# Finer hand-over of a feed-forward beside chains and attention, other leads at two borders, and a forward transform by pairs of slabs

## The chip, the cores and the metric

The kernel runs on one core of a Trainium2 chip. A core has a matrix engine (TensorE, PE in the profile; its weight loads are listed apart as PEld), a vector engine (DVE), a scalar engine (ACT), GpSimd (POOL) and SyncE (SP), which issues most of the transfers. Each engine works through its own queue of instructions in order and waits at semaphores for the others. The metric is the time of one execution on the device in microseconds (us); lower is better.

## The reference

The input x has 4 batches, 512 time steps (T) and 128 x 64 = 8192 features (D), in float32. Two layers follow each other. Cut to what is computed:

```
# layer 0, for each batch
xn = layernorm(x)                                 # over D
k, v, r = xn @ Wk, xn @ Wv, sigmoid(xn @ Wr)      # 64 states
s[t] = decay * s[t-1] + k[t] * v[t]               # a scan over time
x  = x + (r * s) @ Wo
x  = x + gelu(conv(layernorm(x)) + freq_b)        # 3 taps over the 128, 64 x 64 channels
x  = x + layernorm(causal_conv(layernorm(x)))     # 3 taps over time, per feature
x  = x + gelu(x @ W1 + b1) @ W2 + b2              # 64 -> 256 -> 64
# layer 1, for each batch
trend = moving_average(x, 25)                     # over time, ends repeated
xs    = rfft(x - trend)[:128]                     # over time
ys    = einsum(xs, w_real + i * w_imag)           # a 128 x 128 complex matrix per channel
out   = trend + irfft(ys)
```

## The kernel before

**Layer 0** keeps features on the 128 partitions and the 512 time steps along the free axis. A batch has 64 chunks of 128 features, handled in 32 pairs (`NPR`). The work of a batch is written as Python generators, which emit instructions and yield a weight after each step:

- J, `project`: products with Wk, Wv, Wr for all pairs (L407), and the row statistics on DVE (L339).
- Z, `scan`: a chain of short steps, each of which needs the result of the one before. Two rows of scale and mean are spread over the partitions (`rows`, L241 on PE, L285 on ACT), then k and v (L468, L472), r (L476), the scan, and two products (L494, L502/L503) for the next statistics, which end in a power on POOL (L233).
- A, `attend_and_convolve`: two more rows, then for each pair the product with Wo and the sum with x (L527, L529, L533), the convolution (L548 to L563), and sums for the next norm (`add_up`, L251).
- C, `convolve_time`, O, `open_feed`: the causal convolution and its norm; its rows are again chains. `convolve_ahead` does the first 14 pairs of the next batch's convolution early, within F (L611 to L630).
- F, `feed_forward`: for each pair four quarters. `widen(i, q)` is one quad of four 64x64 matmuls (L730) and a GELU on ACT (L735). `narrow(i, q)` is a quad (L743) that accumulates over the quarters into two PSUM banks; after the fourth quarter DVE adds the residual (L756). `store` transposes a finished pair (eight 128x128 transposes, L762), ACT copies it out (L770/L775) and POOL stores every second one (L771). `residual` and `add_residual` (L689, L690, L698, L701) prepare the pair after next.

A step that belongs to a chain yields `CHAIN` (6.0). F yields once per pair.

What TensorE does in which order is fixed by the program (`manual_schedule`); the other engines are ordered by a scheduler that starts from the program's order. `in_turn` sets this order: it walks through eight couples of generators, and takes the next step from the one that is behind. `leads` holds, for each border between couples, by which share of a couple the second generator is to be ahead, and is interpolated in between:

```
((0, (O, 0.05), (F, 0.95)), (2, (J, 0.88), (Z, 0.12))),   # couple 2
((1, (C, 1.0)), (2, (A, 1.0))),                           # couple 3
((1, (O, 0.05), (F, 0.95)), (3, (J, 0.88), (Z, 0.12))),   # couple 4
((2, (C, 1.0)), (3, (A, 1.0))),                           # couple 5
((2, (O, 0.05), (F, 0.95)), (3, (C, 0.95), (O, 0.05))),   # couple 6
((3, (F, 1.0)), (3, (nothing, 1.0))),                     # couple 7
```

A may run three steps beside a running F; at its fourth it is held until F is done, because both need the same PSUM bank.

**Layer 1** takes the batches in twos. For each: `transform` of both, `mix`, `invert` of both. `transform` walks over 16 slabs of 512 features (`SL`). A slab is loaded as `xin`, 128 partitions by four blocks of 512 (L921, five buffers). DVE forms sum and difference of its halves (`uv`, L938) and sum and difference of the first (`ev`, L943). PE multiplies the difference with `dftd` (L947, 128x64 tiles), `ev` with `dftv` (L954, 128x32 tiles), and 24 rows from both ends of time, `edge`, with `dfte` (L961, 24 rows, 64 columns). `edge` is loaded by two POOL transfers (L932, L933) and doubled by ACT (L934). ACT copies the two PSUM banks to `xf` (L963). `mix` (L981, L985) needs all slabs of both batches. The pools give `edge`, `uv0`, `uv1` and `ev` two buffers each, and each of the two PSUM names `a` and `b` four banks.

Of the kernel before, what the change touches and what calls it, by code (L numbers as in the profile page):

```python
# [10 lines left out]
F32 = mybir.dt.float32  # L11
AF = mybir.ActivationFunctionType
ALU = mybir.AluOpType
# [66 lines left out]
def layer0(ctx, tc, dram, x, xt, vecs, wkvr, wo, wdec, wconv, fbias, w1, fb1, w2, fb2, x4):  # L80
# [236 lines left out]
    free_s = [True]  # L317
    feeding = [False]
    held = [False]
    unscanned = [True]  # L320


# [389 lines left out]
    def feed_forward(b):  # L712
# [8 lines left out]
        def unit():  # L721
            turn[0] ^= 1
            return two(ps_m, "m") if turn[0] else c_bank()

        def widen(i, q):
            x3 = x3s[i]
            pm = unit()
            for h in range(2):
                for j in range(2):
                    nc.tensor.matmul(  # L730
                        pm[halves[j], h, :], lhsT=w1_sb[halves[h], q * H : (q + 1) * H], rhs=x3[halves[h], j, :],
                        start=True, stop=True,
                    )
            mid = mids[i, q] = bk.tile([P, 2, SL], F32, tag="mid", name="mid", bufs=4)
            nc.scalar.activation(mid, pm, AF.Gelu_apprx_tanh, bias=fb1_sb[:, q : q + 1])  # L735

        def narrow(i, q):
            if q == 0:
                sums2[i] = of_p(), ps_s.tile([P, SL], F32, tag="s", name="pb")
            mid = mids.pop((i, q))  # L740
            for h in range(2):
                for j in range(2):
                    nc.tensor.matmul(  # L743
                        sums2[i][j][halves[h], :], lhsT=w2_sb[halves[j], q, :], rhs=mid[halves[j], h, :],
                        start=q == 0, stop=q == 3,
                    )
            if q < 3:
                return
            x3 = x3s.pop(i)
            if lag > 1:  # L750
                pair = spare("wx", 4 * S + SL)[:, :, 0:SL]
                x4s[i] = [pair[:, j, :] for j in range(2)]
            else:
                x4s[i] = [bk.tile([P, SL], F32, tag="x4t", name="x4t", bufs=3) for _ in range(2)]
            for j, pa in enumerate(sums2.pop(i)):
                nc.vector.scalar_tensor_tensor(x4s[i][j], pa, fb2_sb, x3[:, j, :], ALU.add, ALU.add)  # L756
# [18 lines left out]
                nc.scalar.copy(o, pt)  # L775

        early = None
        widen(0, 0)
        widen(0, 1)
        for i in range(NPR + lag):  # L780
            if i >= lag:
                store(i - lag)
            if i < NPR:
                widen(i, 2)
                narrow(i, 0)
                widen(i, 3)
                narrow(i, 1)
                if i + 2 < NPR:
                    coming = residual(b, i + 2)
                if i + 1 < NPR:  # L790
                    widen(i + 1, 0)
                narrow(i, 2)
                if i + 1 < NPR:
                    widen(i + 1, 1)
                if i + 2 < NPR:
                    x3s[i + 2] = add_residual(b, i + 2, *coming)
                narrow(i, 3)
            if b + 2 < B and i > 1:
                early = early or convolve_ahead(b + 1, lambda: unit()[:, 0, :])
                next(early, None)  # L800
            yield 9.0 * (NPR + 1) / (NPR + lag)
        feeding[0] = False


# [5 lines left out]
    def run(b, stages):  # L810
        for stage, share in stages:
            for weight in stage(b):
                yield BLOCKED if weight == BLOCKED else weight * share / whole[stage]

    def in_turn(leads, *pairs):
        at, running = [0.0, 0.0], [None, None]
# [54 lines left out]
def layer1(ctx, tc, x4, wri, dftv, dftd, dfte, idfte, idfto, avg, avgh, out):  # L871
# [53 lines left out]

    def transform(b, xf):

        for s in range(NS):
            c = slice(s * SL, (s + 1) * SL)
            xin = slab(b, s)  # L930
            edge = io.tile([P, SL], F32, tag="edge", name="edge")
            nc.gpsimd.dma_start(edge[0:HALO, :], x4[b][0:HALO, c])  # L932
            nc.gpsimd.dma_start(edge[HALO : 2 * HALO, :], x4[b][T - HALO : T, c])  # L933
            nc.scalar.copy(edge[32 : 32 + 2 * HALO, :], edge[0 : 2 * HALO, :])  # L934
            uv = []
            for op in (ALU.add, ALU.subtract):
                t = io.tile([P, 2, SL], F32, tag=f"uv{len(uv)}", name="uv")
                nc.vector.tensor_tensor(t, xin[:, 0:2, :], xin[:, 2:4, :], op)  # L938
                uv.append(t)
            pf = [bank("a"), bank("a")]  # L940
            ev = io.tile([P, 2, SL], F32, tag="ev", name="ev")
            for k, op in enumerate((ALU.add, ALU.subtract)):
                nc.vector.tensor_tensor(ev[:, k, :], uv[0][:, 0, :], uv[0][:, 1, :], op)  # L943
            for i in range(2):
                for r in range(2):
                    h = 1 - r
                    nc.tensor.matmul(  # L947
                        pf[r][h * H : (h + 1) * H, :], lhsT=dftd_sb[:, i, r, :], rhs=uv[1][:, i, :],
                        start=(i == 0), stop=False,
                    )  # L950
            for k in range(2):
                for r in range(2):
                    q = r * H + k * H // 2
                    nc.tensor.matmul(  # L954
                        pf[r][q : q + H // 2, :], lhsT=dftv_sb[:, k, r, :], rhs=ev[:, k, :], start=True, stop=False
                    )
            for r in range(2):
                at = slice(32 * r, 32 * r + 2 * HALO)
                for h in range(2):
                    hs = slice(h * H, (h + 1) * H)  # L960
                    nc.tensor.matmul(pf[r][hs, :], lhsT=dfte_sb[at, hs], rhs=edge[at, :], start=False, stop=True)  # L961
            for r in range(2):
                nc.scalar.copy(by_c(xf[:, r, c]), by_n(pf[r]))  # L963

    def mix(xf):

# [93 lines left out]
def _constants():  # L1060
# [28 lines left out]
    for j, s in enumerate(tiles):  # L1089
# [77 lines left out]
```

## Time and profile before

| | us |
|---|---|
| median of three runs (range) | 3747.47 (3742.09 to 3767.47) |
| profiled execution | 3753.95 |
| its span in the profile | 3752.0 |
| TensorE busy | 3572.1 (95%) |
| VectorE busy | 2676.7 (71%) |
| ScalarE busy | 1762.1 (47%) |
| GpSimd busy | 512.5 (14%) |

Moved through DMA: 913.39 MB, 243 GB/s over the span. The mean granted TensorE clock is 0.975.

Busy time is the union of an engine's instructions; for TensorE the ends are modelled, and a matmul that runs at half clock counts as busy for twice as long. A line of the busy view by stretches gives the stretch, its length, busy us and number of instructions of each engine, the granted clock, the mean busy share of the 16 DMA engines and GB/s. A line of the waits gives who waited for whom, us in total, how often, and the longest. A line of the timeline gives start, duration, engine, line of the code, what is written from what, tile, shape and number of records; a float32 matmul has two records. Behind it, in brackets, stands how long the engine was idle before and what released it.

### The profile page before, as it was taken

How to read it: one execution, taken by the hardware profiler on the slowest of the kernel's cores; microseconds unless marked ns; L12 is line 12 of the kernel's file. 1: busy time of each engine (PE TensorE's matmuls, PEld its weight loads, DVE VectorE, ACT ScalarE, POOL GpSimd, SP SyncE). 2: the span in 40 equal slices, each digit the busy share in tenths (PEclk: the TensorE clock that was granted, in tenths of full speed). 3: DMA queues.
4: the chain of work that ended last, by engine and by line, in shares of the span. 5: the costliest groups of instructions: out<-in, count | busy, mean ns of one | idle time of the engine just before them, and what ended most of it. 6: DMA issues, size and time to landing. Idle time of an engine off the chain costs nothing. (4 is left out here: it accounts for less than half of the span.)

```text
span 3752.0 us, 52992 instructions
## 1 busy us (share of the span) xinstructions
PE 3572.1 (95%) x20041; PEld 1376.3 (37%) x20041; DVE 2676.7 (71%) x3498; ACT 1762.1 (47%) x2299; POOL 512.5 (14%) x782
## 2 busy tenths in 40 slices
PE   9989999999998999999899899999989999999998
PEld 4433322234333223433322333333323833327533
DVE  4445669977776895777689699846667277882677
ACT  0023346656665565666556578868844200142100
POOL 0000012210111221011122121100012000131010
PEclk9999999999998999999889999999999999999999
DMA  9867657787883787788478577645577478983687
GB/s 314 271 211 245 230 187 252 260 275 269 292 286 135 260 286 277 259 292 291 144 249 282 198 256 259 223 159 192 193 247 243 154 247 293 326 277 139 212 289 264
DMA packets 429206, 913.39 MB, mean 243 GB/s; under 512 B 33240, under 2 KB 83608, under 8 KB 424856
## 3 DMA queue, kind: packets, MB, share of 16 engines
q1 hardware_dynamic: 351024, 636.87, 51.6%
q0 software_dynamic: 75776, 271.62, 20.0%
q8 instruction: 160, 2.62, 0.3%
q10 hardware_dynamic: 2152, 1.51, 0.1%
q14 instruction: 94, 0.77, 0.1%
HBM read 641.37 MB, written 268.50 MB: 243 GB/s over the span
## 5 line engine op out<-in xcount | busy, mean ns | idle before, releaser
L743 PE MATMUL p<-mid,w_sb 64*64 64x512 f32 x2048 | 559.1, 596 | 15.5 <-DVE wx L756 14.3
L743 PE MATMUL pb<-mid,w_sb 64*64 64x512 f32 x2048 | 531.6, 596 | 0.7 <-DVE wx L756 0.7
L735 ACT ACTIVATE mid<-c,fb_sb 128x1024 f32<-128x1024 f32 x256 | 284.4, 1111 | 91.4 <-PE c L730 90.9
L735 ACT ACTIVATE mid<-m,fb_sb 128x1024 f32<-128x1024 f32 x256 | 284.8, 1112 | 88.6 <-PE m L730 87.3
L730 PE MATMUL c<-x,w_sb 64*64 64x512 f32 x2016 | 280.8, 610 | 16.1 <-ACT mid L735 11.9
L730 PE MATMUL m<-x,w_sb 64*64 64x512 f32 x2016 | 280.7, 609 | 6.7 <-ACT mid L735 4.5
L743 PEld LDWEIGHTS p<-mid,w_sb 64*64 64x64 f32 x2048 | 158.7, 135 | 287.8 <-issue 248.9
L407 PE MATMUL a<-xp,wx 128*128 128x512 f32 x512 | 238.7, 609 | 0.5 <-DVE me L268 0.5
L1012 ACT COPY two<-a 128x512 f32<-128x512 f32 x64 | 37.5, 586 | 426.6 <-PE a L1007 426.6
L1035 PE MATMUL b<-xin,avg_sb 128*128 128x512 f32 x512 | 230.8, 593 | 3.1 <-DVE xin L1041 3.1
L1041 DVE TENSOR_TENSOR xin<-b,pm 128x512 f32<-128x512 f32 x256 | 159.0, 683 | 97.8 <-PE b L1038 82.8
L568 ACT ACTIVATE sq<-x 128x1024 f32<-128x1024 f32 x128 | 135.0, 1055 | 173.4 <-DVE x L565 173.4
L623 DVE SCALAR_TENSOR_TENSOR to<-kd,vec,to 128x510 f32<-128x510 f32 (+1 forms) x272 | 197.1, 742 | 12.5 <-ACT to L619 11.2
L698 ACT ACTIVATE kd<-kd,vec 128x512 f32<-128x512 f32 x256 | 192.8, 803 | 3.1 <-DVE kd L690 3.1
L917 DVE COPY xf<-b 128x256 f32<-128x256 f32 x128 | 54.3, 424 | 185.4 <-PE b L981 173.3
L251 PE MATMUL st<-x,ones 128*32 128x512 f32 x512 | 168.9, 605 | 11.5 <-DVE x L565 11.5
L529 DVE TENSOR_TENSOR x<-a,xp 128x1024 f32<-128x1024 f32 x128 | 156.0, 1218 | 32.7 <-PE a L527 30.5
L623 DVE SCALAR_TENSOR_TENSOR z<-x,vec,z 128x511 f32<-128x511 f32 x240 | 175.9, 744 | 4.4 <-ACT z L619 2.8
L938 DVE TENSOR_TENSOR uv<-xin 128x1024 f32<-128x1024 f32 x128 | 154.6, 1224 | 32.5 <-PE a L947 15.6
L701 DVE TENSOR_TENSOR x<-kd,kx 128x1024 f32<-128x1024 f32 x126 | 154.0, 1222 | 32.5 <-ACT kd L698 32.5
L527 PE MATMUL a<-rst,wo_sb 64*128 64x512 f32 x512 | 150.7, 663 | 25.8 <-DVE x L529 22.5
L756 DVE SCALAR_TENSOR_TENSOR x4t<-p,fb_sb,x 128x512 f32<-128x512 f32 x64 | 47.9, 748 | 177.2 <-PE pb L743 177.1
(259 smaller groups left out, 6849.8 us busy)
## 6 DMA issues: line engine op xcount, KB each, us to landing
xp<-in_xt SPq DMA_DIRECT2D x256, 512.0 KB
xin<-x SPq DMA_DIRECT2D x128, 1024.0 KB
kh<-to SPq DMA_DIRECT2D x156, 512.0 KB
x<-x POOLq DMA_DIRECT2D x128, 512.0 KB, 4.4
kx<-x SPq DMA_DIRECT2D x128, 512.0 KB
x<-ob POOLq DMA_DIRECT2D x64, 1024.0 KB, 8.3
out<-xin POOLq DMA_DIRECT2D x64, 1024.0 KB, 6.3
x<-x SPq DMA_DIRECT2D x96, 512.0 KB
```

What stands on the lines that cost most here:

```text
L251: nc.tensor.matmul(st[32 * q : 32 * q + 32, :], lhsT=ones, rhs=src[:, j, :], start=first, stop=last,)
L407: nc.tensor.matmul(pa[:, k, :], lhsT=wq[:, j, k * P : (k + 1) * P], rhs=xp[:, j, :], start=first and j == 0, stop=last and j == 1,)
L529: nc.vector.tensor_tensor(x1, at, xp, ALU.add)
L623: tap = nc.vector.scalar_tensor_tensor(to[:, j, k:], xr[:, j, : SL - k], vec[:, w, c], to[:, j, k:], ALU.mult, ALU.add)
L698: tc.keep_in_program_order(nc.scalar.activation(d[:, j, :], d[:, j, :], AF.Identity, bias=vec[:, B4, c], scale=vec[:, G4, c]))
L701: nc.vector.tensor_tensor(x3, d, x2, ALU.add)
L730: nc.tensor.matmul(pm[halves[j], h, :], lhsT=w1_sb[halves[h], q * H : (q + 1) * H], rhs=x3[halves[h], j, :], start=True, stop=True,)
L735: nc.scalar.activation(mid, pm, AF.Gelu_apprx_tanh, bias=fb1_sb[:, q : q + 1])
L743: nc.tensor.matmul(sums2[i][j][halves[h], :], lhsT=w2_sb[halves[j], q, :], rhs=mid[halves[j], h, :], start=q == 0, stop=q == 3,)
L938: nc.vector.tensor_tensor(t, xin[:, 0:2, :], xin[:, 2:4, :], op)
L1035: nc.tensor.matmul(po[j], lhsT=avg_sb[:, j, :], rhs=xin[:, j, :], start=True, stop=False)
L1041: nc.vector.tensor_tensor(by_n(xin[:, j, :]), by_n(po[j]), by_c(pm[j % 2][:, j // 2, :]), ALU.add)
```

## The change

- **F by quarters.** The steps of a pair are the same, with `residual` now before the quarter's `narrow`. F collects weight in `done` by quarters of 2.25 and yields at the end of a pair, or after each quarter as long as the set `narrowly` isn't empty. `run` puts a stage in that set when it yields `CHAIN` or when it is A, and takes it out at another weight or at its end.
- **Leads.** At the borders before couple 3 and before couple 5 the second generator (A of batch 2 and of batch 3) is to be 0.1 ahead in place of 0.04 and 0.02.
- **Transform.** The loop goes over pairs of slabs. The loads and the DVE sums of both are emitted, then the `dftd` matmuls of both, the `dftv` matmuls of both, the `edge` matmuls of both, and four copies. One `edge` tile holds both slabs' rows, at partitions 0 and 64, so the four groups of 24 rows start at 0, 32, 64 and 96; the constant `dfte` is doubled to 128 rows for this. The difference is formed before the sum. Groups use the banks `a` and `b` in turn, four banks each.

```diff
+    narrowly = set()
 ...
         early = None
+        done = 0.0
+        quarter = 2.25 * (NPR + 1) / (NPR + lag)
         widen(0, 0)
         widen(0, 1)
         for i in range(NPR + lag):
             if i >= lag:
                 store(i - lag)
-            if i < NPR:
-                widen(i, 2)
-                narrow(i, 0)
-                widen(i, 3)
-                narrow(i, 1)
-                if i + 2 < NPR:
-                    coming = residual(b, i + 2)
-                if i + 1 < NPR:
-                    widen(i + 1, 0)
-                narrow(i, 2)
-                if i + 1 < NPR:
-                    widen(i + 1, 1)
-                if i + 2 < NPR:
-                    x3s[i + 2] = add_residual(b, i + 2, *coming)
-                narrow(i, 3)
-            if b + 2 < B and i > 1:
-                early = early or convolve_ahead(b + 1, lambda: unit()[:, 0, :])
-                next(early, None)
-            yield 9.0 * (NPR + 1) / (NPR + lag)
+            for q in range(4):
+                done += quarter
+                if i < NPR:
+                    if q < 2:
+                        widen(i, q + 2)
+                    elif i + 1 < NPR:
+                        widen(i + 1, q - 2)
+                    if i + 2 < NPR and q == 1:
+                        coming = residual(b, i + 2)
+                    if i + 2 < NPR and q == 3:
+                        x3s[i + 2] = add_residual(b, i + 2, *coming)
+                    narrow(i, q)
+                if q == 3 and b + 2 < B and i > 1:
+                    early = early or convolve_ahead(b + 1, lambda: unit()[:, 0, :])
+                    next(early, None)
+                if q == 3 or narrowly:
+                    yield done
+                    done = 0.0
 ...
             for weight in stage(b):
+                if weight == CHAIN or stage is attend_and_convolve:
+                    narrowly.add((stage, b))
+                elif weight != BLOCKED:
+                    narrowly.discard((stage, b))
                 yield BLOCKED if weight == BLOCKED else weight * share / whole[stage]
+            narrowly.discard((stage, b))
 ...
-            (0.12, 0.12, 0.08, 0.04, 0.08, 0.02, -0.05, 0.08, 0.0),
+            (0.12, 0.12, 0.08, 0.1, 0.08, 0.1, -0.05, 0.08, 0.0),
 ...
-        for s in range(NS):
-            c = slice(s * SL, (s + 1) * SL)
-            xin = slab(b, s)
+        for g in range(NS // 2):
             edge = io.tile([P, SL], F32, tag="edge", name="edge")
 ...
+            uv, ev, pf = [], [], []
+            for k in range(2):
+                s = 2 * g + k
+                c = slice(s * SL, (s + 1) * SL)
+                xin = slab(b, s)
+                q = k * H
+                nc.gpsimd.dma_start(edge[q : q + HALO, :], x4[b][0:HALO, c])
+                nc.gpsimd.dma_start(edge[q + HALO : q + 2 * HALO, :], x4[b][T - HALO : T, c])
+                nc.scalar.copy(edge[q + 32 : q + 32 + 2 * HALO, :], edge[q : q + 2 * HALO, :])
+                u = io.tile([P, 2, SL], F32, tag="uv0", name="u")
+                v = io.tile([P, 2, SL], F32, tag="uv1", name="v")
+                nc.vector.tensor_tensor(v, xin[:, 0:2, :], xin[:, 2:4, :], ALU.subtract)
+                nc.vector.tensor_tensor(u, xin[:, 0:2, :], xin[:, 2:4, :], ALU.add)
+                t = io.tile([P, 2, SL], F32, tag="ev", name="ev")
+                for i, op in enumerate((ALU.add, ALU.subtract)):
+                    nc.vector.tensor_tensor(t[:, i, :], u[:, 0, :], u[:, 1, :], op)
+                uv.append(v)
+                ev.append(t)
+                pf.append([bank("ab"[g % 2]), bank("ab"[g % 2])])
+            for k in range(2):
+                for i in range(2):
+                    for r in range(2):
+                        h = 1 - r
+                        nc.tensor.matmul(
+                            pf[k][r][h * H : (h + 1) * H, :], lhsT=dftd_sb[:, i, r, :], rhs=uv[k][:, i, :],
+                            start=(i == 0), stop=False,
+                        )
 ...
+            for k in range(2):
+                for r in range(2):
+                    at = slice(k * H + 32 * r, k * H + 32 * r + 2 * HALO)
+                    for h in range(2):
+                        hs = slice(h * H, (h + 1) * H)
+                        nc.tensor.matmul(
+                            pf[k][r][hs, :], lhsT=dfte_sb[at, hs], rhs=edge[at, :], start=False, stop=True
+                        )
 ...
-        "dfte": dfte.reshape(2 * 32, M),
+        "dfte": np.concatenate([dfte.reshape(2 * 32, M)] * 2),
```

More of the change, by code (lines that the diff above doesn't have):

```diff
@@ L926, in transform @@
     def transform(b, xf):
-        for s in range(NS):
-            c = slice(s * SL, (s + 1) * SL)
-            xin = slab(b, s)
+        for g in range(NS // 2):
             edge = io.tile([P, SL], F32, tag="edge", name="edge")
[L932 to L950, printed above, removed]
@@ new lines, in transform @@
+            for k in range(2):
[7 more added lines that the diff above has]
+            for k in range(2):
+                for i in range(2):
+                    for r in range(2):
+                        q = r * H + i * H // 2
+                        nc.tensor.matmul(
+                            pf[k][r][q : q + H // 2, :], lhsT=dftv_sb[:, i, r, :], rhs=ev[k][:, i, :],
+                            start=True, stop=False,
+                        )
@@ L951, in transform @@
             for k in range(2):
                 for r in range(2):
[L953 to L961, printed above, removed]
@@ L962, in transform @@
-            for r in range(2):
-                nc.scalar.copy(by_c(xf[:, r, c]), by_n(pf[r]))
+                    at = slice(k * H + 32 * r, k * H + 32 * r + 2 * HALO)
+                    for h in range(2):
+                        hs = slice(h * H, (h + 1) * H)
+                        nc.tensor.matmul(
+                            pf[k][r][hs, :], lhsT=dfte_sb[at, hs], rhs=edge[at, :], start=False, stop=True
+                        )
+            for k in range(2):
+                s = 2 * g + k
+                for r in range(2):
+                    nc.scalar.copy(by_c(xf[:, r, s * SL : (s + 1) * SL]), by_n(pf[k][r]))
```

## The prediction

> **What bounds the kernel now.** I began with the page's first two parts.
>
> ```profile
> span 3752.0 us, 52992 instructions
> ...
> PE 3572.1 (95%) x20041; PEld 1376.3 (37%) x20041; DVE 2676.7 (71%) x3498; ACT 1762.1 (47%) x2299; POOL 512.5 (14%) x782
> ...
> PE   9989999999998999999899899999989999999998
> ...
> PEclk9999999999998999999889999999999999999999
> ```
>
> TensorE is the bound: 95% busy, the next engine at 71%. Only two things are left to take from it: its 180 us of idle time, and time in which it is busy but slow. So I asked where the granted clock falls, by stretches of the busy view:
>
> ```profile
> 1150.00:1240.00 90.00, 71.53 (x400) 30.58 (x402) 53.57 (x75) 41.20 (x49) 11.65 (x16) 0.79 0.38 130
> 1800.00:1900.00 100.00, 79.40 (x474) 31.50 (x466) 62.52 (x84) 49.34 (x59) 11.21 (x16) 0.80 0.37 130
> ...
> 2762.00:2893.00 131.00, 129.17 (x768) 30.81 (x764) 112.26 (x125) 55.67 (x94) 36.48 (x70) 0.98 0.92 305
> 3250.00:3387.00 137.00, 133.83 (x770) 31.76 (x768) 113.93 (x128) 56.01 (x96) 39.49 (x73) 0.96 0.87 288
> ```
>
> Columns: stretch, its length, busy us of PE, PEld, DVE, ACT and POOL, granted clock, DMA share, GB/s. The first two are the borders where a feed-forward F ends, the scan Z of a later batch runs and its attention A begins. Idle is 18.5 and 20.6 us. By slices of 10 us, busy time times (1 - clock) is a further 14.3 and 15.5 us. A border thus loses about 33 to 36 us, 69 us for both. The waits of the second border and two rows of its timeline (start, duration) say why:
>
> ```profile
> PE a L494 <- DVE rst L489: 7.1, 1, 7.1
> PE a L241 <- POOL rs L233: 5.2, 2, 3.3
> PE a L468 <- DVE wx L472: 3.4, 1, 3.4
> ...
> 1819.45 1.16 PE L241 MATMUL a<-ident,mean 128*128 128x128 f32 x8
> ...
> 1870.14 2.08 PE L241 MATMUL a<-ident,rs 128*128 128x128 f32 x8 [3.34 <-POOL rs L233]
> ```
>
> Each step of the scan needs a DVE or POOL result of the step before. Two scan steps stand back to back, with the whole pair of F (8.2 us) before or after both. After a gap the same eight transposes take 2.08 in place of 1.16 us.
>
> The last two stretches are the forward transforms of two batches each, 32 slabs in 131.8 us (2761.6 to the mix's first matmul at 2893.3) and in 136.7 us (3250.3 to 3387.0). One slab in the steady part:
>
> ```profile
> 2853.77 1.94 PE L947 MATMUL a<-uv,dftd_sb 128*64 128x512 f32 x8
> ...
> 2855.64 1.07 PE L954 MATMUL a<-ev,dftv_sb 128*32 128x512 f32 x8
> 2855.75 1.22 DVE L938 TENSOR_TENSOR uv<-xin 128x1024 f32<-128x1024 f32 x1 [0.19 <-PE a L947]
> ...
> 2856.63 1.09 PE L961 MATMUL a<-edge,dfte_sb 24*64 24x512 f32 x8
> ...
> 2857.65 1.94 PE L947 MATMUL a<-uv,dftd_sb 128*64 128x512 f32 x8
> ```
>
> Start to start, a slab costs PE 1.87 + 0.99 + 1.02 = 3.88 us, and DVE waits for PE to free `uv`. Where DVE runs freely its slabs start at 2800.76, 2804.36 and 2807.96: 3.60 us. DMA moves 305 GB/s there at share 0.92, and 376 GB/s in the first 20 us of the stage.
>
> **What the Trainium skill says.** "TensorE: Matmul & The Clock Gate", Part 1, has the array at half clock after an idle window of about 3.4 us; 1.16 against 2.08 us agrees. "TensorEngine Tiling (Array Packing)", Key Properties, says that a change of tiling mode drains the array. The trace agrees: quads of one shape follow each other at 0.86 us, and the slab's L954, the same 512 columns, costs 0.99 where shapes change, so about 0.14 us each. The tiling page's list of configurations has eight tiles of 32x64; before shows four of them side by side (8 records of L961 in 1.09 us), not eight.
>
> **Part 1: quarters and leads.** F does the same matmuls; only its hand-over is finer while the partner is in a chain or in A. The planned order of the changed kernel puts this between the steps at both borders (quad w or n: 0.86 us, eight transposes T: 1.05): first row, 2.8 us, second row, 3.4, first k/v, 6.2, second k/v, 3.4, r, 4.5, L494, 6.2, L502, 3.4, row, 6.2, row, 7.9, first L527. Against this the delays of before, from the end of a step to the start of what it frees:
> - k/v to k/v 3.4 (cover 6.2): 0 left. k/v to r 4.1 (3.4): 0.7. r to L494 7.05 (4.5): 2.6.
> - L494 to L502/L503 about 4.5 (6.2): 0. L502 to the row 5.2 (3.4): 1.8. Rows to L527 1.4 or less: 0.
> - Unchanged: first row 1.7 (the scan still follows the last projection at once), one L527 behind L529 1.3, waits for GELU about 2.
> - New: the last T stands right behind the last n and waits for two L756, 1.5; and 10 more changes of tile shape at 0.15, 1.5.
>
> Together 13 us, and 2 for one cold window (the 2.6 could set one off): 15 against 34.5, so **-19.5 per border, -39 for both**. Moved along: A's first three steps with `xp` and `wo_sb` loads on SP, 3 x 2.44 us on DVE (L529, L533) and `scaled` on ACT come into F's tail. Queued behind them are F's last L756 and L735, for which the last n and T wait. DVE is at 63% there, so nothing beyond the 1.5; without that room two adds, 2.4 us a border. DVE and SP also meet J's statistics and loads in another order earlier in F. PE is at 98 to 99% from 900 to 1100, so I take nothing; bounds -3 to +6. In F2 beside C3 a second row comes two quads earlier, before a 3.0 us wait for GELU at 2154: zero, +-4.
>
> **Part 2: two slabs together.** Same matmul count. Per pair of slabs: eight concurrent edge matmuls in one slot take away 1.02, and the modes change 3 times, not 6: 3 x 0.14. PE: 2 x 3.88 - 1.02 - 0.42 = 6.3 us. If eight tiles don't run together it is 7.3. DVE keeps its instructions: 2 x 3.60 = 7.2. So DVE becomes the bound either way, and 0.28 us a slab is what the steady part can give.
>
> First stage: the second slab lands at 2766.1 as before; 31 slabs x 3.60 to 2877.7; then the last quads 2.0 and four evacuations 2.5 (two before; here the mix waits for them, +1.2): 2882, **-11**. Second: 32 x 3.60 from 3249 plus 4.5 is 3369 without loads in the way. The first 12 slabs, though, ran at 4.05 us with DMA share about 1.0, late output stores among it; there I take no gain, which leaves about **-8**. The edge tile is now issued two groups ahead (14 us in place of 7), so the late edges (L961 of 1.5 to 1.7 us, 2.5 us of wait) go; that is inside the 3.60. Bounds -28 to 0: DVE's full pace throughout, or loads that hold everything. POOL issues four edge DMAs of 0.5 us per 7.2 us, as before; `dfte` doubles by 16 KB: nothing. The wait of 8.6 us at the stage's start (the first `xin` lands at 2759.0) stays.
>
> **Sum.** 39 + 11 + 8 = 58 us. The profiled execution ran 3753.95 us (span 3752.0, 2 us around it): 3696. It lies 6.5 us over the median of the runs, 3747.5, less 58: 3689.5. I say **3692**.
>
> **Rivals.**
> 1. *Only one part pays.* Chains are bound by DVE's order, since DVE was over 90% busy around 1250 to 1300: each row and scan step waits behind L611/L623/L701 whatever PE does, half of 39 remains; or the transform is held by DMA and gives 0 to 5. Against it: delays were measured with that same queue, and 376 GB/s was reached. 20 to 37 us less: about **3718**.
> 2. *Slower: the pair of slabs serializes.* `uv0`, `uv1` and `ev` have two buffers, and a group now takes both. If DVE can't write the next `v` until PE has done both dftd blocks, and PE can't begin before both `v` exist, they take turns: 7.2 + 2 x 1.87 = 10.9 a group against 8.2 to 8.5 now, 32 x 2.5 = +80; minus 39, **3788**. The point that decides: the next `v` must find `v` of the group before free. By the planned order (u u v v, four ev) DVE returns to `v` 7.2 us later, and PE is done with it 3.7 us after it starts, so about 2 to 3 us remain. It needs PE to lag more than that.
> 3. *The chains overlap as planned and nothing stays cold*: 25 per border and 28 in the transforms: **3670**.
>
> That the change does not do what it says is excluded by the planned order.
>
> **How the numbers follow.** Forecast 0.58, rival 1 0.22, rival 2 0.07, rival 3 0.13. The range 3662 to 3732 takes in the forecast, rival 3 and nearly all of rival 1; outside it lies rival 2 and some of the tails. A measurement can tell about 1% (37 us) from no change: below 3710 lie the forecast, rival 3 and a little of rival 1, **0.73**; within, **0.19**; slower **0.08**.
>
> **What would show it.** Right: at the two borders no PE wait over 4 us, clock above 0.9, the wait for `rst` down to 2 to 3 us; transform groups 7.2 to 7.4 us apart, with PE waiting for DVE `v` or `ev`, eight edge matmuls in about 1.1 us, and the two stages near 121 and 128 us. Wrong: groups over 7.8 us apart, DVE waiting for PE dftd, `xin` as the last releaser over the whole stage, or waits on L756 and GELU at the borders that add up to more than 15 us.

## The result, and the profile after

The changed kernel takes 3746.7 us (median of 20 runs, 3723.6 to 3749.1), the kernel before 3757.8 in the runs beside it (20 runs, 3742.1 to 3773.7). The ratio over all runs is **0.9963, 95% interval 0.9949 to 0.9977**: 14 us less (the medians are 11 apart), within the 1% that the prediction called no change. Forecast were 3692 us, a gain of 58 us, counted from earlier runs of the kernel before. In layer 0 most lines are one further now: L756 is L757, L762 is L763, L356 is L357. In the transform, DVE's sums L938 and L943 are L948, L949 and L952, the edge loads L932 and L933 are L943 and L944, L947 is L960, L954 is L968, L961 is L977, and the sign flip of the mix's weights, L974, is L994. The kernels with freed edges, below, have one line more again from the edge loads on. F0 is F of batch 0, A2 is A of batch 2, and so on.

The page after, first two parts (busy us and share of the span; then busy tenths and granted clock in 40 slices):

```profile
span 3745.2 us, 53017 instructions
...
PE 3536.6 (94%) x20041; PEld 1368.8 (37%) x20041; DVE 2669.1 (71%) x3498; ACT 1759.4 (47%) x2299; POOL 522.6 (14%) x782
...
PE   9999999999998999999999989999988999989998
...
PEclk9999999999999999999999999999999999999999
```

PE is busy 35.5 us less than before, at nearly the same mean clock (0.974), but the span fell by 6.8: idle time took the place of slow and needless work. The busy view by the same four stretches as before (length, busy us of PE, PEld, DVE, ACT, POOL, clock, DMA share, GB/s):

```profile
1150.00:1240.00 90.00, 71.17 (x482) 27.31 (x481) 52.23 (x69) 48.61 (x55) 7.46 (x12) 0.89 0.41 138
1800.00:1900.00 100.00, 86.88 (x601) 32.85 (x601) 69.59 (x91) 60.91 (x70) 13.13 (x17) 0.93 0.46 153
2762.00:2893.00 131.00, 112.69 (x772) 32.71 (x773) 111.83 (x128) 55.00 (x96) 40.63 (x67) 0.93 0.94 315
3250.00:3387.00 137.00, 120.04 (x806) 39.63 (x803) 111.79 (x132) 56.08 (x99) 41.92 (x71) 0.94 0.87 294
```

The first border is still idle for 18.8 us (18.5 before), the second for 13.1 (20.6). The clock there rose from 0.79 and 0.80 to 0.89 and 0.93. Part of such a rise can be chance: the kernel with the new transform alone (below), whose layer 0 is that of before, shows 0.85 and 0.83. The transforms now have idle time that they did not have: 18.3 us in the third row, 1.8 before.

By PE's own events I measure four stretches: from F0's first quad to the end of C1 (the last matmul of its statistics; it holds the first border), from there to the end of C2 (the second border), and the two transforms, from the first `dftd` matmul to the mix's first matmul.

| us | F0 to C1's end | to C2's end | transform 1 | transform 2 |
|---|---|---|---|---|
| before | 645.3 | 658.1 | 131.8 | 136.7 |
| after | 652.5 | 653.7 | 127.3 | 126.6 |

One caution about such figures. The stretch from the start to F0's first quad (820.5 before) took 820.0 to 832.2 us in kernels whose program there is the same, and the kernel with the new transform alone has 639.6 and 655.8 in the first two columns. A few us of one profile decide nothing; the timed ratios and single waits do.

What TensorE waits for at the two borders, the first border and then the second:

```profile
PE c L763 <- DVE x4t L757: 9.1, 5, 4.3
PE m L763 <- DVE x4t L757: 7.0, 4, 5.3
PE a L241 <- POOL rs L233: 1.9, 1, 1.9
PE a L528 <- DVE x L530: 1.6, 2, 1.3
PE a L495 <- DVE rst L490: 1.0, 1, 1.0
```

```profile
PE c L763 <- DVE x4t L757: 6.0, 4, 2.3
PE m L763 <- DVE x4t L757: 2.0, 3, 0.9
...
PE a L241 <- POOL rs L233: 1.6, 1, 1.6
PE a L495 <- DVE rst L490: 0.8, 1, 0.8
```

The chain's own waits went as planned: `rst` from 7.1 to 0.8 us, the rows from 5.2 to 1.6 at the second border. In their place stand the transposes of a finished pair, which wait for its sums `x4t` at nearly every pair's end: 16.1 and 8.0 us. The kernel before has no such wait at the borders. The longest is in this piece of the timeline of after, DVE and PE together:

```profile
1156.42 0.69 DVE L474 TENSOR_TENSOR wx<-wx,rm 128x512 f32<-128x512 f32 x1
...
1156.88 0.60 PE L744 MATMUL pb<-mid,w_sb 64*64 64x512 f32 x2
...
1161.43 0.55 DVE L357 TENSOR_SCALAR wx<-wx,vec 128x192 f32<-128x192 f32 x2 [4.33 <-DMA wx<-in_wkvr]
1161.90 0.74 DVE L757 SCALAR_TENSOR_TENSOR x4t<-p,fb_sb,x 128x512 f32<-128x512 f32 x1
...
1162.79 1.09 PE L763 MATMUL m<-ident,x4t 128*128 128x128 f32 x4 [5.31 <-DVE x4t L757]
...
1165.53 1.99 PE L731 MATMUL c<-x,w_sb 64*64 64x512 f32 x8
```

The pair's last matmul ends at 1157.5. DVE could add the residual then, but its queue holds ahead of L757 the scaling of a *later projection's* weights, L357, and that waits 4.33 us for their load. TensorE stands for 5.31 us, and the next quad runs at half speed (1.99 in place of 1.09); I call such matmuls cold.

The end of the first transform, POOL and then PE:

```profile
2870.50 9.79 POOL L994 TENSOR_SCALAR w<-w 128x256 f32<-128x256 f32 x4 [6.62 <-DVE ev L952]
2880.24 0.55 POOL L943 DMA_DIRECT2D edge<-x  x1
```

```profile
2874.00 1.11 PE L977 MATMUL a<-edge,dfte_sb 24*64 24x512 f32 x16
2875.51 3.65 PE L960 MATMUL b<-v,dftd_sb 128*64 128x512 f32 x16 [0.40 <-DVE v L948]
2879.09 1.92 PE L968 MATMUL b<-ev,dftv_sb 128*32 128x512 f32 x16
2886.58 3.24 PE L977 MATMUL b<-edge,dfte_sb 24*64 24x512 f32 x16 [5.56 <-DMA edge<-x]
2891.50 1.22 PE L1001 MATMUL b<-xf,w 128*128 128x256 f32 x2 [1.68 <-ACT xf L983]
2892.53 1.05 PE L1005 MATMUL b<-xf,w 128*128 128x256 f32 x2
```

The steady part is better than forecast: a group each 6.95 us (7.2 to 7.4 were forecast), sixteen edge records in 1.11 us. But the last group's four edge loads stand behind four sign flips on POOL's queue, are issued at 2880.2 to 2881.8, and PE waits 5.56 us. The edge matmuls then take 3.24 in place of 1.11, and the mix starts at 1.05 per step in place of 0.59. The second stage ends in the same way, with 5.04 us.

### The profile page after: what moved, and what is told of

Its sections match the earlier page's. It is cut to its first block, busy times and chain, and to the rows that moved or that the text cites. A ratio compares the mean times of both kernels' runs of the same rounds, so it can differ in the third digit from the quotient of the medians.

```text
span 3745.2 us, 53017 instructions
## 1 busy us (share of the span) xinstructions
PE 3536.6 (94%) x20041; PEld 1368.8 (37%) x20041; DVE 2669.1 (71%) x3498; ACT 1759.4 (47%) x2299; POOL 522.6 (14%) x782
## 5 line engine op out<-in xcount | busy, mean ns | idle before, releaser
L567 POOL DMA_DIRECT2D x<-x x128 | 93.6, 731 | 560.4 <-DVE x L566 544.7
L757 DVE SCALAR_TENSOR_TENSOR x4t<-p,fb_sb,x 128x512 f32<-128x512 f32 x64 | 47.9, 748 | 170.6 <-PE pb L744 168.1
```

## The experiments

My theory after reading both profiles: the parts do what they were made for, and four things give it back: (a) nothing covers a pair's end since chain steps no longer stand there, (b) DVE's order makes two of these waits long, (c) the leads of 0.1 cost something by themselves, (d) the last edge loads are late. Rivals are named with each. In what follows us are worked out as (1 - ratio) times 3757, and the difference of two kernels is that of two such figures; where their intervals overlap, the time alone does not tell the two apart.

**The three parts alone.** Each is the kernel before with one part of the change's diff: `transform` with the doubled `dfte`; `narrowly`, the loop by quarters and `run`; or

```diff
-            (0.12, 0.12, 0.08, 0.04, 0.08, 0.02, -0.05, 0.08, 0.0),
+            (0.12, 0.12, 0.08, 0.1, 0.08, 0.1, -0.05, 0.08, 0.0),
```

> The kernel before, with the new transform of two slabs alone. Theory A (the late last edges eat half of the transform's gain): the stages are 131.8 and 136.7 us in the kernel before and lost about 5 us each to late edges and about 5 more to the cold clock in the kernel after, so this one is 8 to 14 us faster than before (ratio 0.9963 to 0.9979), and all of the change's gain is in this part. Theory B (the gain seen in the second layer is variation of one execution, and loads set the pace): 0 to 4 us. In the profile A expects groups 7.0 us apart, and at the end of each stage about 5 us of wait for the edge tile.

> The kernel before, with the hand-over by quarters alone: old leads, old transform. Theory A (the quarters shorten the chains at the borders by as much as they lose to transposes behind the last narrow quad, and the larger leads cost about 9 us in each couple of A and C): without the leads the couples A2/C1 and A3/C2 keep their 230 and 222 us, and the borders gain a part: 5 to 15 us faster than before (0.9960 to 0.9987). Theory B (the new wait of the transposes for x4t is all that counts, the leads are harmless): 0 to 8 us slower.

> The kernel before, with the two leads of 0.1 alone: whole pairs, old transform. Theory A (the leads cost DVE time in the couples of A and C, some 9 us each, since C starts later behind A and DVE is first starved and then full): 8 to 18 us slower than before (1.0021 to 1.0048). Theory B (the leads only move work from the couple to the border): within 4 us of before. In the profile A expects the couples A2/C1 and A3/C2 at 236 to 240 and 228 to 231 us.

Measured: transform **0.9962** (0.9949 to 0.9976), quarters **0.9961** (0.9949 to 0.9974), leads **1.0043** (1.0027 to 1.0058): -14, -15 and +16 us, sum -13, and the whole change has -14. Each is near the far end of what theory A gave, the transform just past it. The transform alone has stages of 127.0 and 127.7 us and the same late edges (5.4 the longest). By these sums the whole gain that is left is that of the transform; quarters and leads cancel.

The leads' profile doesn't put their 16 us in one place. The couples that the expectations name, taken from A's first convolution matmul to A's last statistics, last 230.6 and 222.1 us before, 230.3 and 221.5 with quarters alone, 236.9 and 226.7 with leads alone and 239.8 and 231.0 after; but with the new leads the last transposes of F fall into them, so this does not part lost time from moved work. One wait that kernels with old leads don't show is there twice, in this kernel as in the kernel after (page of the kernel with the leads alone, waits; here L356 is the scaling of the projection's weights and L407 the projection):

```profile
PE a L241 <- POOL rs L233: 23.2, 8, 5.3
...
PE a L407 <- DVE wx L356: 8.6, 2, 4.3
```

and the row's wait, 17.5 us before, is 23.2: the row behind L502/L503 now waits 5.3 us at each border.

**Old leads in the kernel after.** The last line of the diff above, turned round.

> The kernel after with the two old leads (0.04 and 0.02): quarters and new transform stay. Theory A (the parts add up: quarters about -14, transform about -14, leads about +16 against before): 12 to 18 us less than the kernel after, 26 to 32 less than before (0.9915 to 0.9931). Theory B (the leads lose only where whole pairs are handed out; with quarters they give the chains their cover): 0 to 8 us more than the kernel after, 6 to 14 less than before.

**0.9945** (0.9926 to 0.9964), 21 us less than before and 7 less than after: between the two theories, with intervals that overlap. That the leads cost less with quarters than with whole pairs is likely but not shown; that they pay, as B has it, these runs give no sign of.

**The freed edges.** The kernel after with one line that chooses the queue for the last group of a stage:

```diff
+            late = nc.scalar if b % 2 and g >= NS // 2 - 1 else nc.gpsimd
-                nc.gpsimd.dma_start(edge[q : q + HALO, :], x4[b][0:HALO, c])
+                late.dma_start(edge[q : q + HALO, :], x4[b][0:HALO, c])
```

(and the same for the second load).

> The kernel after, with the edge loads of the last group of each transform stage issued from ScalarE's queue, where no sign flip of the mix's weights stands ahead of them. Theory A (these loads come late because they are queued behind the sign flips on GpSimd, and the gap also cools the clock at the mix's start): the wait of 5.0 to 5.6 us at the end of each stage falls under 1.5 us, and with the cold matmuls behind it 7 to 10 us per stage come back: 14 to 20 us less than the kernel after, about 28 to 33 less than before (0.991 to 0.9927). Theory B (another input of the last group, v or the slab's load, is nearly as late): the wait changes its name, 0 to 5 us less than the kernel after.

**0.9909** (0.989 to 0.9928): 34 us less than before, 20 less than after. The stages take 118.9 and 120.0 us. PE at the first stage's end in this kernel:

```profile
2878.22 1.93 PE L969 MATMUL b<-ev,dftv_sb 128*32 128x512 f32 x16
2880.08 1.11 PE L978 MATMUL b<-edge,dfte_sb 24*64 24x512 f32 x16
2882.86 0.70 PE L1002 MATMUL b<-xf,w 128*128 128x256 f32 x2 [1.67 <-ACT xf L984]
```

No wait before the edge matmuls, full speed, and the mix begins warm (0.70, 0.67, then 0.59 per step). (d) is shown.

**Why the sign flip takes so long.** A flip lasts 0.41 us at the median of the 64, but the first of each stage after lasts 8.68 and 7.67 us; before, the longest is 1.49. "SBUF — State Buffer", section "Who interferes with whom", of the Trainium skill says that a DVE instruction with two SBUF inputs contends with a GpSimd instruction that reads SBUF, not with one that only writes it. In the transform after, DVE runs just such sums (L948, L949, L952) without a gap, and the long flip, 2870.50 to 2879.18, ends 0.3 us after the last of them. So the flip was replaced by a fill, which leaves the change of sign out; the mix then computes something else in the same number of steps:

```diff
-                nc.gpsimd.tensor_scalar(t, t, -1.0, 0.0, ALU.mult, ALU.add)
+                nc.gpsimd.memset(t, 0.0)
```

> The kernel after, with GpSimd filling the mix's weights with zero where it flips their sign: the same places, written and not read (the sign flip is left out, so the mix's result is another). The order on GpSimd's queue is that of the kernel after. Theory A (the flip reads SBUF and is locked out as long as DVE runs additions of two SBUF inputs back to back; the first one lasted 8.7 and 7.7 us and ended as DVE did): a write alone isn't held, takes under 1 us, and the last edge loads are in time: 12 to 20 us less than the kernel after, near the kernel with the freed edges (0.990 to 0.993). Theory B (GpSimd is slowed by something else, such as its own queue or the weights' load): it lasts as long, and the time stays within 4 us of the kernel after (0.995 to 0.9974).

**0.9937** (0.9915 to 0.996), 10 us less than after, with intervals that overlap; A asked for 12 at least, so the size is just under its range. The mechanism shows in POOL's timeline of this kernel:

```profile
2877.50 0.56 POOL L994 MEMSET w<- 128x256 f32 x2 [6.65 <-DVE ev L952]
2880.48 0.57 POOL L994 MEMSET w<- 128x256 f32 x2 [2.42 <-DMA w<-in_wri]
2881.18 0.50 POOL L943 DMA_DIRECT2D edge<-x  x1
```

Each fill takes 0.31 us while DVE is as full as before, the wait for the edges is gone from both stages, and the first stage takes 121.2 us. POOL still waits for the weights' load and for `ev` ahead of the edges, since the queue's order is the same, and the edges come barely in time: the last edge matmuls take 1.98 and 1.59 us in place of 1.11, the mix waits 2.6 us for `xf` (1.7 in after and with freed edges) and again starts cold. That would be the other half of the freed edges' 20 us; no run shows it by itself.

**Transposes moved.** The kernel after, with `store` taken from the head of the loop to behind the first narrow quad:

```diff
-            if i >= lag:
-                store(i - lag)
                     narrow(i, q)
+                if q == 0 and i >= lag:
+                    store(i - lag)
```

> The kernel after, with the transposes of a finished pair moved behind the first wide and narrow quads of the next pair. Theory A (PE stands still because the last sums of a pair leave PSUM late, and the next pair's first narrow quad needs the same bank): the wait moves from the transposes to that narrow quad and loses only the 0.9 us of the wide quad ahead of it at each of some ten pair ends; 3 to 8 us less than the kernel after. Theory B (the transposes' place is the whole cost): the 15 and 8 us of waits at the two borders go with their cold windows, 14 to 22 us less.

**1.0123** (1.01 to 1.0147): 46 us more than before, 60 more than after. Both theories missed. The borders went as A said (the wait for `x4t` by transposes fell to 6.4 us, and the narrow quad has a new one of 5.7), but F lost elsewhere. Waits of the stretch 820 to 2800 in this kernel:

```profile
PE c L731 <- ACT mid L736: 13.6, 11, 1.4
PE m L731 <- ACT mid L736: 13.2, 13, 1.4
...
PE p L744 <- DVE x4t L757: 5.7, 3, 2.9
```

The transposes take one of the two PSUM names `m` and `c` in turn with the wide quads. Between the wide quads of quarters 2 and 3 they push the second of these back to the bank whose GELU still runs: 26.8 us of such waits, 8.5 after. From F2's first wide quad to F3's last it takes 654.4 us, 615.5 after. Of those 39 us 16 are idle time; for the rest PE is busy longer (600.5 us, 577.6 after), and the trace shows first narrow quads of a pair that take 1.7 us in place of 1.0. The place at the head of the pair was part of the banks' rhythm; the experiment does not tell the price of the transposes' place by itself.

**DVE's order.** One argument keeps the first scaling of a later projection in program order on DVE:

```diff
-            scale_weights(0, ws[0])
+            scale_weights(0, ws[0], True)
```

> The kernel after, with the scaling of a later projection's first weights held in program order on DVE, so that it can't stand ahead of the sums x4t that leave PSUM. Theory A (DVE's order makes the two long waits of 5.3 and 4.3 us at the first border: the scaling waits there 4.3 and 3.6 us for its weights): both fall under 2 us and the half-speed quads behind them go, 8 to 12 us less than the kernel after. Theory B (DVE is late there for another reason, or the scaling is late where it belongs): the waits keep their size or a wait of the projection takes their place, within 3 us of the kernel after.

**0.9978** (0.9967 to 0.9988), 6 us more than after, with intervals that overlap: by the time, neither. But from the projection's end to A2's first convolution matmul it has 73.6 us (84.5 after), the long waits are gone (6.5 and 2.0 us left, 2.3 the longest), and instead the projection of batch 2 starts late, with a new wait of 4.1 us at its first matmul, for which the profile names no cause; F0's first quad comes at 834.6, 9.5 us later than after. More than that wait I could not place there, and kernels with one and the same program up to that quad came to it at up to 832.2. So the next run holds the order for the last batch alone, `b == 3`, on top of the freed edges:

> The kernel with the freed last edge loads and the leads of 0.1, and the scaling of the first weights held in program order for the last batch's projection alone. Theory A (held for all, it gave 11 us at the first border and lost them at the start of the projection of batch 2, which came 7.5 us later): now the border's gain stays, 8 to 12 us less than the kernel with the freed edges (0.9877 to 0.9888 against before). Theory B (what the border gains is lost in the attention and convolution behind it, where DVE sets the pace): within 3 us of that kernel (0.9901 to 0.9917).

**0.9886** (0.987 to 0.9903): 9 us less than with the freed edges alone, as A, with intervals that overlap a little. By the waits (b) is shown: the longest at a pair's end falls from 5.0 to 2.3 us; its price in time is 9 us, not sharply known.

**All that paid, with old leads** (quarters, transform, freed edges, leads 0.04 and 0.02), and the same with the order held for the last batch:

> Quarters, new transform, old leads, and the last edge loads of each transform stage on ScalarE's queue. Theory A (all parts add up): quarters -14, transform -14, freed edges -20: 44 to 52 us less than before (0.9862 to 0.9883). Theory B (the gains share waits, above all the clock's cold windows): 34 to 42 less.

> The combined kernel with old leads and quarters, and the last projection's first scaling held in program order. There that scaling waits only once, 3.3 us, at the first border, ahead of the second sum r and of x4t. Theory A (DVE's order makes this wait): 3 to 6 us less than the combined kernel (0.9883 to 0.9891). Theory B: the sigmoid behind r stays the last to come, and nothing changes: within 2 us (0.9894 to 0.9904).

**0.9899** (0.9877 to 0.992) and **0.9887** (0.9868 to 0.9906). The first, 38 us, is B's size and not A's 44. It is near the 41 that the kernel after with old leads (21) and the freed edges (20) give together; that shared cold windows are the reason for the rest, as B has it, is not shown. The second can't be told from the first by time; in its profile the transposes' wait for `rg`, the gate r of the scan, at the first border fell from 5.9 to 2.1 us, and the one of 5.4 for `x4t` stayed.

**Halves in place of quarters.** A chain step then stands in the middle or at the end of a pair, never just ahead of its last quarter:

```diff
-                if q == 3 or narrowly:
+                if q == 3 or q == 1 and narrowly:
```

> The combined kernel with old leads, but the pair handed out in halves, not quarters, while the partner is in a chain: a chain step then stands at the middle or at the end of a pair. Theory A (a pair's end needs something for PE to do while the sums leave PSUM, and a chain step's matmuls there are the cover that the quarters took away): the waits of the transposes at the two borders, 12 and 9 us, fall below 5 us each, and the chain's own waits rise by less: 4 to 12 us less than the combined kernel (0.9867 to 0.9888). Theory B (the chain needs the quarters' spread): 0 to 8 us more (0.9899 to 0.992).

> Freed last edge loads, leads of 0.1, the last projection's first scaling held in program order, and halves in place of quarters. Theory A (the two causes of waits at a pair's end, DVE's order and the lack of cover, are separate): 10 to 20 us less than the kernel with the freed edges alone (0.9856 to 0.9882). Theory B (either one is enough, or the chains lose what the pair ends gain): 0 to 8 us less (0.9888 to 0.9909).

With old leads **0.9889** (0.9872 to 0.9905), 4 us less than the combined kernel, the low end of A, with intervals that overlap, though only at the second border is the wait gone (0.9 us left, 9.0 in the combined kernel); at the first 11.9 stay, the longest 6.0. With the freed edges, leads of 0.1 and the last projection's order held, **0.985** (0.9833 to 0.9867): 56 us less than before and 22 less than with the freed edges alone. This is more than either theory gave; the kernel, the fastest here, runs 3703.0 us (3698.9 to 3706.8). Its waits at the first border and its two stretches:

```profile
PE c L763 <- DVE x4t L757: 2.9, 1, 2.9
PE a L241 <- POOL rs L233: 1.9, 1, 1.9
PE a L528 <- DVE x L530: 1.3, 1, 1.3
PE m L763 <- DVE x4t L757: 1.1, 2, 0.9
```

```profile
1150.00:1240.00 90.00, 83.44 (x582) 31.12 (x571) 65.96 (x79) 57.59 (x68) 13.29 (x19) 0.96 0.55 187
1800.00:1900.00 100.00, 93.37 (x637) 34.78 (x637) 75.96 (x90) 63.55 (x76) 16.11 (x22) 0.97 0.54 184
```

Idle 6.6 us at both, clock 0.96 and 0.97. Against the kernel with quarters, freed edges and held order (0.9886) the halves give 14 us, with intervals apart, and the waits for `x4t` fall from 8.5 to 4.0 us at each border: (a) is shown. (a) and (b) are two causes.

**What is left open** was asked with two more: the fastest kernel with old leads, and the kernel after with halves and the held order, but late edges.

> The fastest kernel so far (halves, freed last edges, scaling of the last projection held in order) with the old leads of 0.04 and 0.02. Theory A (a larger lead puts attention steps between the chain steps and pays once the pair ends no longer wait): 6 to 16 us more than with 0.1 (0.9866 to 0.9893 against before). Theory B (the lead costs what it did with whole pairs, and the gain was in the halves): 3 to 10 us less (0.9823 to 0.9842).

> The kernel after with halves in place of quarters and the last projection's first scaling held in order; the last edge loads stay late. Theory A (the waits at the pair ends took the gain of the first part, apart from the transform): 18 to 26 us less than the kernel after (0.9894 to 0.9915 against before). Theory B (without the freed edges the two layers' gains are the same thing seen twice): 0 to 10 us less.

**0.9867** (0.9845 to 0.9889) and **0.99** (0.9885 to 0.9915). The first lies 6 us over the fastest, A's low end, with intervals that overlap; in the stretches where the leads act the two are alike (637.6 and 645.6 us; 638.4 and 645.4), although the windows at the borders are not. With the old leads they are

```profile
1150.00:1240.00 90.00, 72.78 (x478) 30.20 (x476) 63.63 (x84) 48.99 (x57) 11.71 (x16) 0.92 0.45 155
1800.00:1900.00 100.00, 88.05 (x540) 33.61 (x539) 74.99 (x98) 55.64 (x66) 14.15 (x20) 0.88 0.48 161
```

that is, idle for 17.2 and 12.0 us, where the fastest kernel has 6.6 twice. So the new leads fill the borders and lose it again elsewhere; the projection's two waits of 4.3 us, which the fastest kernel has too, are one such place. Whether the leads matter in the end these runs can't tell.

The second is 24 us less than after: its stretches are 638.2 and 645.4, against 652.5 and 653.7. With it the first part gives 24 us, where 39 were forecast and quarters with leads gave about nothing: most of the missing gain was lost at the pairs' ends.

| us | F0 to C1's end | to C2's end | transform 1 | transform 2 | ratio |
|---|---|---|---|---|---|
| after, old leads | 642.1 | 653.0 | 126.8 | 127.8 | 0.9945 |
| freed edges | 651.2 | 654.6 | 118.9 | 120.0 | 0.9909 |
| and held order | 644.9 | 650.6 | 119.2 | 121.2 | 0.9886 |
| and halves | 638.4 | 645.4 | 119.1 | 117.8 | 0.985 |

## Why the prediction was wrong

**The chain delays against their cover: right.** My sum left 2.6 us of the wait for `rst`, 1.8 of that of the row behind L502/L503 and 0.7 of that for `wx`. Of the first 1.0 and 0.8 us are left at the two borders, of the others nothing; the first row, taken as unchanged at 1.7, waits 1.9 and 1.6.

**"New: the last T stands right behind the last n and waits for two L756, 1.5": this step failed.** I read it once per border. The planned order has it at almost every end of a pair while the quarters are handed out (nine waits at the first border, seven at the second; a pair's two halves can wait one each). Before, by the program's order, a chain step, with its whole matmuls, or the projection's four stood between; I listed what stands between chain steps and did not ask what stands between the last quad of a pair and what needs its sums, though both sums have one PSUM bank each. It cost 16.1 and 8.0 us, and the cold quads behind them.

**"DVE is at 63% there, so nothing beyond the 1.5": failed.** A busy share says nothing on the head of an in-order queue. DVE was idle for 4.33 and 3.55 us with L757 ready behind an instruction that waited for a load. My outer bound, two adds or 2.4 us a border, was for a busy DVE. Held in order, the longest wait fell to 2.3 us, and the time by about 9.

**"DVE and SP also meet J's statistics and loads in another order ... I take nothing": failed.** The projection has two new waits of 4.3 us for its scaled weights, 8.6 us together, against nothing and a bound of +6. They come with the leads: the kernel with these alone has them, those with the old ones don't.

**"Moved along: A's first three steps": mis-sized.** I gave the leads nothing of their own. With whole pairs they cost 16 us; with quarters it is 7, with intervals that overlap.

**The price of a border: taken from the wrong thing.** I counted idle and slow time in a fixed window as time that the kernel would save. By that count, redone from the busy lines above (idle, and busy time times 1 - clock), the fastest kernel loses about 10 us at each border, 50 less than before for both, yet its first part gives some 22 us; with old leads the windows still lose about 23 us each, and the two stretches are just as short. What is gained inside such a window may only have moved out of it.

**The transform: the mechanism was right, the bound (DVE) too, the steady pace a little better.** -11 was forecast for the first stage, and -4.5 measured, since 8 us went at its end; freed of that it is 118.9, against the forecast 121. For the second -8 was forecast and -10.1 measured, which is luck: the sum was wrong in two places. Its own figures, twelve slabs at 4.05, twenty at 3.60 and 4.5 us from 3249 on, end at 3374, 13 us earlier than before and not 8; and the late edges took back 6.6 us of a gain that was larger than either, since with freed edges the stage is 120.0. The failed step is **"POOL issues four edge DMAs of 0.5 us per 7.2 us, as before ...: nothing"**. I counted the DMAs and not what else is in POOL's queue. Before, one sign flip pair stood between the edges of two slabs (0.8 to 2.8 us for two); now four stand ahead of all edges of the last group, and a DVE without gaps holds the first of them. The phrase "so the late edges go" was wrong for the same reason.

**Rivals.** The nearest is the first, only one part pays, 3718; it named DVE's order as the bound, and that is part of the cause, but the place was the pair's sums, not the rows. The serializing of the slabs didn't come: DVE never waited for PE's `dftd` in the steady part. My list of signs had the right alarm, waits on L756 and GELU at the borders of more than 15 us; I gave it too little weight. That the fastest kernel, 56 us under before, comes near the forecast 58 is no proof of my sum: by the sums above about 34 of it are the transform's, where 19 were forecast, and 22 the first part's, where it was 39.

## What to carry to other kernels

When steps are woven more finely to cover a chain, look at what the old, coarse order covered by accident: here the end of a pair, where PSUM must be emptied before PE can go on. For each in-order queue ask what stands at its head and what that waits for, not how busy it is. And when an engine is brought to 100%, ask which other engine lived on its gaps. A window of a profile shows where time goes, not what a change will save.

## What was not expected of the hardware

A GpSimd instruction that reads SBUF, started beside sums of two SBUF inputs on DVE, did not get in between two of them: it lasted 8.68, 7.67 and (with freed edges) 8.81 us, until DVE's run of them ended, where 0.41 is its median; a fill of the same places took 0.31 us throughout. In all thirteen kernels here with the new transform and the flip, the first flip of each stage lasted 7.4 to 8.8 us. The skill's page, section "SBUF: two separate sides", has the lock for the length of one instruction; here it held over a whole back-to-back run of DVE. The kernel before shows that this is not all: there the longest flip, 1.49 us, ended 0.3 us after one sum, and the next sum had started without a gap and took 0.88 us in place of 0.68. What let that flip in between, and none after, is not shown.

Eight groups of edge matmuls (sixteen records of 24 rows by 64 columns, 512 long) ran in 1.11 us, where four took 1.09 before. After the gap of 5.56 us the same sixteen took 3.24 us, and the mix's step 1.05 in place of 0.59.
